# Attention block on one core: the weights of a Strassen group in one tile of seven blocks, in place of two tiles of four and three

## The chip, the cores and the metric

The kernel runs on 1 core of one Trainium2 chip. The metric is the device time in microseconds; the time of a kernel is the median of its runs.

## The reference

`x` has 16 images of 512 channels and 32 x 32 = 1024 positions, float32 throughout. One layer of self-attention with a group norm and a residual is computed:

```python
xn = group_norm(x, 8 groups, eps=1e-5) * norm_gamma + norm_beta
q, k, v = split(einsum('oc,bchw->bohw', qkv_w, xn) + qkv_b)      # each 512 x 1024 an image
# 4 heads of 128 channels
attn = softmax(q k^T / sqrt(128))                                 # 1024 x 1024 a head
out = attn v                                                      # back to 512 x 1024
out = einsum('oc,bchw->bohw', proj_w, out) + proj_b
return x + out
```

## The kernel before

**Attention.** The loop runs over steps: image `b`, head `h` of 4, key block `j` of 8 (128 keys). In a step TensorE makes a score tile of 128 keys by 1024 queries in two halves (`s`, L741), ScalarE takes its exponential (`p`, L746), VectorE adds it to a running sum (`tot`, L752 and L754), and TensorE adds V times `p` to the output's PSUM tile (`po`, L836), one step behind. At the end of a head VectorE makes the softmax's denominators (`denominators`, L763 to L777), whose inverses go to DRAM (`row`) and come back on all partitions (`rinv`); a head later VectorE multiplies the output by them (`divide`).

**Projections.** The q and k weights of two heads (a "pair"), the v weights and the output projection are each multiplied by Strassen's method in the Winograd form, on two levels: seven outer products, and in each of them seven inner ones. `two_levels` makes the units. The outer products come in four groups, `OUTER = ((1, 5), (2, 6), (7, 4), (3,))`; a group makes its one or two outer products side by side. In a group the inner products run in this order, the first operand of each being one block of weights (128 x 128 for each product of the group) and the second a block of x or of the heads' outputs (or a sum of such blocks, `in_t1` to `in_t4`, made by VectorE at L522):

```python
FACTORS = {
    1: ("a11", "b11"), 2: ("a12", "b21"), 3: ("s4", "b22"), 4: ("a22", "t4"),
    5: ("s1", "t1"), 6: ("s2", "t2"), 7: ("s3", "t3"),
}
ORDER = (1, 2, 6, 5, 7, 4, 3)
```

The products of one accumulator are copied by ScalarE (`kept_copy`, L448) and joined by VectorE (`out_`, L557), then combined over the groups (L593) and finished. The four sites are q and k of pair 0, of pair 1, v, and proj. Their groups are staggered: group 1 starts four units after group 0, and so on.

**Where the units stand.** `plan_head` lays them between the attention steps. In image b's head 0 stands pair 1 of the same image, in head 1 the output projection of the image before (and the load, the statistics and the normalisation of the next image's x), in head 2 pair 0 of the next image, in head 3 v of the next image, in seven of the eight key blocks. The Tile framework's scheduler orders the instructions of each engine from this; each engine then works in that order and waits on semaphores.

**Weights.** `group_weights` gives a group its blocks. In image 0 it makes them from the raw weights: blocks a11 to a22 by DMA or, for the outer sums, by VectorE, then s1 to s4 by VectorE. Then it writes them to DRAM (`kept`), and every later image reads them back with `nc.sync.dma_start`, whose queue (SP's) also carries the loads of v's kept sums `v_t` (L511, L588). The tile pool has two buffers of each tile, so a group's load waits until TensorE has read the last block of the same tile two groups before. A block's place is given by `SLOTS`; s3 takes the place of a21.

**Other DMA queues.** On POOL's stand the loads of x, of the residual (`y<-in_x`), the stores of the output (`out_y<-y`), the stores of the kept sums (`kept_t<-qk_t`) and the transposition of v by way of DRAM (`vd<-vu`, `v<-vd`); on ScalarE's `row` and `rinv`.

Of the kernel before, what the change touches and what calls it, by code (L numbers as in the profile page):

```python
# [10 lines left out]
F32 = mybir.dt.float32  # L11
# [5 lines left out]
P = 128  # L17
# [71 lines left out]
def attention_block(  # L89
# [52 lines left out]
FACTORS = {  # L142
    1: ("a11", "b11"), 2: ("a12", "b21"), 3: ("s4", "b22"), 4: ("a22", "t4"),
    5: ("s1", "t1"), 6: ("s2", "t2"), 7: ("s3", "t3"),
}


SLOTS = {
    "a11": (0, 0), "a12": (0, 1), "s1": (0, 2), "s2": (0, 3),
    "a21": (1, 0), "s3": (1, 0), "a22": (1, 1), "s4": (1, 2),  # L150
}
PARTS = (4, 3)
KC = 2
Q = 256

# [4 lines left out]
def fast_path(ctx, tc, x, sources, out, consts, flag, dims):  # L160
# [6 lines left out]
    nc = tc.nc  # L167
# [8 lines left out]
    wpool = ctx.enter_context(tc.tile_pool(name="w", bufs=2))  # L176
# [12 lines left out]
    kept = ctx.enter_context(tc.tile_pool(name="kept", bufs=1, space=DRAM))  # L189
# [120 lines left out]
    def load_block(dst, src):  # L310

        to = dst.rearrange("p (r k) d -> p r k d", k=KC)
        for k in range(KC):
            nc.sync.dma_start(
                to[:, :, k, :], src[ts(k, P), :].rearrange("p (r d) -> p r d", d=P)
            )

    stage, store = {}, {}
    for site in (*range(PAIRS), "proj", "v"):
        for g, group in enumerate(OUTER):  # L320
            for t, m in enumerate(PARTS):
                store[site, g, t] = kept.tile(
                    [P, len(group), m, P], F32, name=f"kept_{site}_{g}_{t}"
                )

    store["last"] = kept.tile([P, 8, HALF], F32, name="kept_last")

# [22 lines left out]

    def group_weights(site, g, first):


        group = OUTER[g]
        n = len(group)
        w = [
            wpool.tile([P, 2, m, P], F32, tag=f"w{t}", name=f"w{t}_{site}_{g}")
            for t, m in enumerate(PARTS)
        ]
        if not first:  # L360
            for t in range(2):
                nc.sync.dma_start(w[t][:, :n], store[site, g, t])
            return w
        st, raw = stage[site], raw_blocks(site)
        for i, p in enumerate(group):
            name = FACTORS[p][0]
            for t in range(2):
                rows = w[t][:, i, 0:2, :]
                flat = rows.rearrange("p s d -> p (s d)")
                if name in raw:  # L370
                    nc.sync.dma_start(
                        rows, raw[name][:, ts(t, P)].rearrange("(k p) d -> p k d", p=P)
                    )
                    continue

                def of(m):
                    return st[m][:, ts(t, 2 * P)]

                if name == "s1":
                    nc.vector.tensor_add(flat, of("a21"), of("a22"))  # L380
                elif name == "s2":
                    nc.vector.tensor_sub(flat, of("s1"), of("a11"))
                elif name == "s3":
                    nc.vector.tensor_sub(flat, of("a11"), of("a21"))
                else:
                    nc.vector.tensor_sub(flat, of("a12"), of("s2"))
            if site == "proj":
                for t in range(2):
                    nc.sync.dma_start(
                        store["last"][:, p, ts(t, 2 * P)],  # L390
                        w[t][:, i, 0:2, :].rearrange("p s d -> p (s d)"),
                    )

        def at(m):
            t, slot = SLOTS[m]
            return w[t][:, :n, slot, :]

        nc.vector.tensor_add(at("s1"), at("a21"), at("a22"))
        nc.vector.tensor_sub(at("s3"), at("a11"), at("a21"))
        nc.vector.tensor_sub(at("s2"), at("s1"), at("a11"))  # L400
        nc.vector.tensor_sub(at("s4"), at("a12"), at("s2"))
        for t in range(2):
            nc.sync.dma_start(store[site, g, t], w[t][:, :n])
        return w

    wv = {}
# [25 lines left out]
    def run(units):  # L432
        for u in units:
            u()
# [49 lines left out]
    def two_levels(name, site, b, blocks, finish, sums="make"):  # L484
# [10 lines left out]
        def group_units(g):  # L495
            group = OUTER[g]
            n = len(group)
            have = haves[g]

            def weights():  # L500
                have["w"] = group_weights(site, g, b == 0 and site in range(PAIRS))

            def sum_tile(h, m):
                haves[h][m] = tpool.tile(
                    [P, 2, Q], F32, tag=f"in_{m}", name=f"{name}_{h}_{m}"
                )
                return haves[h][m][:, : len(OUTER[h])]

            def load(h, m):
                if sums == "load" and h < len(OUTER):  # L510
                    nc.sync.dma_start(sum_tile(h, m), inner_kept[b, h, m])  # L511

            def inner_sum(m):
                if sums == "load":
                    return
                sum_tile(g, m)
                a, c = {
                    "t1": ("b12", "b11"), "t2": ("b22", "t1"), "t3": ("t2", "b11"),
                    "t4": ("b21", "t2"),
                }[m]  # L520
                for i in range(n):
                    nc.vector.tensor_sub(have[m][:, i, :], inner(i, a), inner(i, c))  # L522
                if sums == "keep":
                    t = dpool.tile([P, n, Q], F32, tag=f"{m}_{g}", bufs=1, name=f"kept_{m}_{g}")
                    inner_kept[b, g, m] = t
                    nc.gpsimd.dma_start(t, have[m][:, :n])  # L526

            def inner(i, m):
                if m[0] == "t":
                    return have[m][:, i, :]  # L530
                outer = blocks()[FACTORS[group[i]][1]]
                return outer[int(m[1]) - 1][:, ts(int(m[2]) - 1, Q)]

            def mm(acc, j, first):
                an, bn = FACTORS[j]
                t, slot = SLOTS[an]
                for i in range(n):
                    nc.tensor.matmul(  # L538
                        acc[:, ts(i, Q)], have["w"][t][:, i, slot, :], inner(i, bn),
                        start=(first and i == 0), stop=True, skip_group_check=True,  # L540
                    )

            def out_(which, a, c=None):
                row, half = int(which[1]) - 1, int(which[2]) - 1
                if g not in R:
                    R[g] = rpool.tile(
                        [P, 2, 2, HALF], F32, tag=f"r{g % 3}", name=f"{name}_r{g}"
                    )
                dst = R[g][:, :n, row, ts(half, Q)]

                def view(t):
                    return t[:, : n * Q].rearrange("p (i q) -> p i q", q=Q)

                if c is None:
                    nc.scalar.copy(dst, view(a))
                else:
                    nc.vector.tensor_add(dst, view(a), view(c))  # L557

            p1, p2, p6, p5, p7, p4, p3 = strassen(f"{name}_{g}", mm, out_, n * Q)

            def unit(*steps):
                def one():
                    for f in steps:
                        f()
                    for _ in range(min(len(pending), 2 if g == len(OUTER) - 1 else 1)):
                        pending.pop(0)()
                return one

            def end():
                combine(g)  # L570
                if g == len(OUTER) - 1:
                    run(pending)
                    pending.clear()


            return [
                unit(weights, lambda: inner_sum("t1"), lambda: inner_sum("t2"), p1),
                unit(lambda: inner_sum("t3"), p2), unit(lambda: inner_sum("t4"), p6),
                unit(lambda: load(g + 1, "t2"), p5), unit(lambda: load(g + 1, "t1"), p7),
                unit(lambda: load(g + 1, "t3"), p4),  # L580
                unit(lambda: load(g + 1, "t4"), p3, end),
            ]
# [17 lines left out]
        def combine(g):  # L600

            if g == 1:
                done("c11", (0, 0), (1, 0))
                add((1, 1), (0, 0), (1, 1))
                add((1, 0), (1, 1), (0, 1))
            elif g == 2:
                add((2, 0), (1, 1), (2, 0))
                done("c22", (2, 0), (0, 1))
                done("c21", (2, 0), (2, 1))
            elif g == 3:  # L610
                done("c12", (1, 0), (3, 0))
# [444 lines left out]
    for s in range(steps + 1):  # L1056
# [14 lines left out]
        for half in range(NH2):  # L1071
# [10 lines left out]
            n = (len(units) + 1) // 2  # L1082
# [137 lines left out]
```

## Time and profile before

| | |
|---|---|
| median of 3 runs | 3298.59 us (3294.85 to 3303.18) |
| the profiled execution's own time | 3294.85 us |
| its span, first to last instruction | 3293.0 us |
| TensorE matmuls busy | 3198.6 us, 97% |
| VectorE busy | 2639.3 us, 80% |
| ScalarE busy | 1443.6 us, 44% |
| GpSimd busy | 525.1 us, 16% |
| mean granted TensorE clock | 0.996 |
| DMA | 530.59 MB, mean 161 GB/s |

One execution was profiled. [...] A float32 matmul appears as two records. In the timeline a row gives the start, the time from the first start to the last end of the records that it merges, the engine, the line, the operation, the operands, and in brackets the idle time before it with what ended it. In the DMA issues a row ends in the size of one and the median time from issue to landing. In the waits a row gives the total, the number and the longest.

### The profile page before, as it was taken

The numbers are of one execution on the slowest core, as the hardware profiler recorded it, in microseconds if no ns is written. First come the engines' busy times: TensorE is split into PE (matmuls) and PEld (weight loads), VectorE is DVE, ScalarE is ACT, GpSimd is POOL, SyncE is SP. The second block draws the span as 40 slices with busy tenths as digits, with TensorE's granted clock in tenths as the row PEclk, the third lists the DMA queues.
The fourth block names the chain that finished last, engine by engine and source line by source line (L and its number), as shares of the span: only waits on it lengthen the run. The fifth ranks groups of instructions, "written<-read, shape, count | busy, mean of one in ns | idle before, by whom it ended". The sixth has DMA issues, their size and how long they took to land.

```text
span 3293.0 us, 34096 instructions
## 1 busy us (share of the span) xinstructions
PE 3198.6 (97%) x10474; PEld 2177.7 (66%) x10474; DVE 2639.3 (80%) x4625; ACT 1443.6 (44%) x2709; POOL 525.1 (16%) x938
## 2 busy tenths in 40 slices
PE   8999999999999999999999999999999999999999
PEld 6566666666666666666666666666666666666664
DVE  8878878778787787878888787887878878788684
ACT  2535435344353443534435354353533535344342
POOL 1011121111211112111121201212012120121100
PEclk9999999999999999999999999999999999999999
DMA  6554554545545455454554545546455463554631
GB/s 206 196 189 152 168 182 139 181 137 178 169 150 174 140 170 166 155 169 142 179 168 156 172 130 183 169 148 182 132 174 172 147 200 124 176 160 154 195 122 40
DMA packets 210539, 530.59 MB, mean 161 GB/s; under 512 B 33072, under 2 KB 66096, under 8 KB 210352
## 3 DMA queue, kind: packets, MB, share of 16 engines
q1 hardware_dynamic: 128992, 276.88, 27.2%
q0 software_dynamic: 67392, 216.07, 20.0%
q10 hardware_dynamic: 13968, 35.41, 3.1%
q8 instruction: 87, 1.43, 0.2%
q14 instruction: 100, 0.82, 0.1%
HBM read 389.56 MB, written 138.67 MB: 160 GB/s over the span
## 4 chain that ended last, share of the span: by engine, by line
issue 38%; PE 37%; DVE 11%; DMA 7%; POOL 5%; ACT 0%; POOLq 0%; SPq 0%; DVEq 0%
PE po L836 10%; PE s L741 10%; PE qk_x L538 5%; DMA vd<-vu 4%; POOL kept_t L526 4%; PE qk_y L538 4%; PE pp_x L538 4%; PE pp_y L538 3%; DMA out_y<-y 2%; DVE xt L277 2%; DMA y<-in_x 1%; DVE tot L754 1%; DVE vu L680 1%; DVE part L765 1%; DVE tt L763 1%
## 5 line engine op out<-in xcount | busy, mean ns | idle before, releaser
L836 PE MATMUL po<-p,v 128*128 128x512 f32 x2048 | 1056.6, 598 | 0.0
L741 PE MATMUL s<-qk,qk 128*128 128x512 f32 x2048 | 1052.8, 596 | 3.3 <-ACT p L746 3.2
L746 ACT ACTIVATE p<-s 128x512 f32<-128x512 f32 x1024 | 609.7, 596 | 851.6 <-PE s L741 810.0
L836 PEld LDWEIGHTS po<-p,v 128*128 128x128 f32 x2048 | 603.2, 303 | 328.2 <-issue 209.0
L754 DVE TENSOR_TENSOR tot<-tot,p 128x1024 f32<-128x1024 f32 x385 | 468.5, 1217 | 164.6 <-ACT p L746 162.6
L741 PEld LDWEIGHTS s<-qk,qk 128*128 128x128 f32 x2048 | 388.6, 191 | 106.4 <-issue 40.0
L538 PE MATMUL qk_x<-qk_t,w 128*128 128x256 f32 x1344 | 363.2, 387 | 43.0 <-DVE qk_t L522 38.6
L538 PEld LDWEIGHTS qk_x<-qk_t,w 128*128 128x128 f32 x1344 | 248.5, 191 | 211.9 <-issue 106.5
L448 ACT COPY qk_u<-qk_x 128x512 f32<-128x512 f32 (+1 forms) x256 | 136.1, 532 | 333.7 <-PE qk_x L538 286.7
L526 POOL DMA_DIRECT2D kept_t<-qk_t x256 | 138.3, 540 | 505.6 <-DVE qk_t L522 455.9
L688 POOL DMA_DIRECT2D vd<-vu x120 | 66.2, 552 | 747.5 <-DVE vu L680 745.8
L557 DVE TENSOR_TENSOR qk_r<-qk_y,qk_u 128x512 f32<-128x512 f32 (+1 forms) x256 | 158.3, 618 | 25.8 <-ACT qk_u L448 19.7
L538 PE MATMUL pp_x<-pp_t,w_proj 128*128 128x256 f32 x630 | 170.7, 387 | 6.4 <-ACT pp_p L448 6.4
L538 PE MATMUL v_x<-v_t,w_v 128*128 128x256 f32 x630 | 166.6, 381 | 0.0
L725 POOL DMA_DIRECT2D out_y<-y x120 | 66.2, 552 | 624.2 <-DVE y L724 591.6
L557 DVE TENSOR_TENSOR v_r<-v_y,v_u 128x512 f32<-128x512 f32 (+1 forms) x120 | 74.5, 621 | 112.5 <-ACT v_u L448 82.3
L538 PEld LDWEIGHTS pp_x<-pp_t,w_proj 128*128 128x128 f32 x630 | 113.9, 190 | 76.3 <-issue 22.5
L538 PEld LDWEIGHTS v_x<-v_t,w_v 128*128 128x128 f32 x630 | 118.5, 190 | 53.6 <-issue 23.0
L538 PE MATMUL qk_y<-x,w 128*128 128x256 f32 x512 | 144.4, 384 | 9.4 <-DVE qk_r L557 9.3
L693 POOL DMA_DIRECT2D v<-vd x240 | 139.9, 590 | 79.3 <-issue 67.1
L752 DVE TENSOR_TENSOR tot<-p,p 128x1024 f32<-128x1024 f32 x64 | 78.3, 1223 | 78.4 <-ACT p L746 78.4
L448 ACT COPY v_u<-v_x 128x512 f32<-128x512 f32 (+1 forms) x124 | 66.2, 534 | 165.1 <-PE v_x L538 126.2
(204 smaller groups left out, 4524.8 us busy)
## 6 DMA issues: line engine op xcount, KB each, us to landing
kept_t<-qk_t POOLq DMA_DIRECT2D x192, 256.0 KB, 3.5
w<-kept SPq DMA_DIRECT2D x90, 512.0 KB, 4.0
v_t<-kept_t SPq DMA_DIRECT2D x180, 256.0 KB, 3.0
w<-kept SPq DMA_DIRECT2D x90, 384.0 KB, 3.8
rinv<-row ACTq DMA_DIRECT2D x63, 512.0 KB, 5.5
x<-in_x POOLq DMA_DIRECT2D x60, 512.0 KB, 4.9
vd<-vu POOLq DMA_DIRECT2D x120, 256.0 KB, 3.4
v<-vd POOLq DMA_DIRECT2D x240, 128.0 KB, 4.5
```

Of the source, the lines that this page charges most:

```text
L448: nc.scalar.copy(t[n][:, :width], t["x"][:, :width])
L526: nc.gpsimd.dma_start(t, have[m][:, :n])
L538: nc.tensor.matmul(acc[:, ts(i, Q)], have["w"][t][:, i, slot, :], inner(i, bn), start=(first and i == 0), stop=True, skip_group_check=True,)
L557: nc.vector.tensor_add(dst, view(a), view(c))
L688: nc.gpsimd.dma_start(rows[which][ts(h, P), :], u)
L693: nc.gpsimd.dma_start(vs[b, pair][ts(q, BLK), half].rearrange("m h (k i) j -> m (h k) (i j)", k=n), rows[which].rearrange("(k m) (q e) -> ...
L725: nc.gpsimd.dma_start(out[b, ts(o, P), ts(half, HALF)], t)
L741: nc.tensor.matmul(sc, ks[b, h][:, ts(j, P)], qs[b, h][:, ts(half, HALF)], start=True, stop=True)
L746: nc.scalar.activation(ps[s][:, ts(half, HALF)], sc, AF.Exp, scale=SCALE)
L752: nc.vector.tensor_add(tot[b, h], ps[s - 1], ps[s])
L754: added[b, h, j] = nc.vector.tensor_add(tot[b, h][:, i], tot[b, h][:, i], ps[s][:, i])
L836: nc.tensor.matmul(po[b, h][:, i], v_block(b, h, j), ps[s][:, i], start=(j == 0), stop=(j == NB - 1),)
```

## The change

The two tiles `w0` and `w1` of a group become one tile `w` of seven blocks. In place of a load of 512 KB and one of 384 KB for a group of two products (half of that for the group of one) there is one load of 896 KB (448 KB) from one DRAM tile; so too for the stores in image 0. The outer sums of image 0 are made in one VectorE instruction of 512 columns in place of two of 256, and the raw blocks are loaded by `load_block`, in two DMAs as before, but cut by rows and not by columns. TensorE's, ScalarE's and GpSimd's instructions are the same in number. The stores of `store["last"]`, two for each block, become one.

```diff
-SLOTS = {
-    "a11": (0, 0), "a12": (0, 1), "s1": (0, 2), "s2": (0, 3),
-    "a21": (1, 0), "s3": (1, 0), "a22": (1, 1), "s4": (1, 2),
-}
-PARTS = (4, 3)
+SLOTS = {"a11": 0, "a12": 1, "a21": 2, "s3": 2, "a22": 3, "s1": 4, "s2": 5, "s4": 6}
...
         for g, group in enumerate(OUTER):
-            for t, m in enumerate(PARTS):
-                store[site, g, t] = kept.tile(
-                    [P, len(group), m, P], F32, name=f"kept_{site}_{g}_{t}"
-                )
+            store[site, g] = kept.tile(
+                [P, len(group), 7, P], F32, name=f"kept_{site}_{g}"
+            )
...
         group = OUTER[g]
-        n = len(group)
-        w = [
-            wpool.tile([P, 2, m, P], F32, tag=f"w{t}", name=f"w{t}_{site}_{g}")
-            for t, m in enumerate(PARTS)
-        ]
+        w = wpool.tile([P, 2, 7, P], F32, tag="w", name=f"w_{site}_{g}")
         if not first:
-            for t in range(2):
-                nc.sync.dma_start(w[t][:, :n], store[site, g, t])
+            nc.sync.dma_start(w[:, : len(group)], store[site, g])
             return w
...
-        for t in range(2):
-            nc.sync.dma_start(store[site, g, t], w[t][:, :n])
+        nc.sync.dma_start(store[site, g], w[:, : len(group)])
         return w
...
             def mm(acc, j, first):
                 an, bn = FACTORS[j]
-                t, slot = SLOTS[an]
                 for i in range(n):
                     nc.tensor.matmul(
-                        acc[:, ts(i, Q)], have["w"][t][:, i, slot, :], inner(i, bn),
+                        acc[:, ts(i, Q)], have["w"][:, i, SLOTS[an], :], inner(i, bn),
                         start=(first and i == 0), stop=True, skip_group_check=True,
                     )
```

In the built program the order of TensorE's instructions in the images from the second on differs in one place an image: in head 2, a score and a weighted sum (half a key block each) stand ahead of the first product of pair 0's group 2, not behind it. ScalarE's order follows by one place; VectorE's and GpSimd's there are the same.

More of the change, by code (lines that the diff above doesn't have):

```diff
@@ L365, in group_weights, with at @@
         for i, p in enumerate(group):
-            name = FACTORS[p][0]
-            for t in range(2):
[L368 to L386, printed above, removed]
-            if site == "proj":
[L388 to L396, printed above, removed]
+            n = FACTORS[p][0]
+            flat = w[:, i, 0:4, :].rearrange("p s d -> p (s d)")
+            if n in raw:
+                load_block(w[:, i, 0:4, :], raw[n])
+            elif n == "s1":
+                nc.vector.tensor_add(flat, st["a21"], st["a22"])
+            elif n == "s2":
+                nc.vector.tensor_sub(flat, st["s1"], st["a11"])
+            elif n == "s3":
+                nc.vector.tensor_sub(flat, st["a11"], st["a21"])
+            else:
+                nc.vector.tensor_sub(flat, st["a12"], st["s2"])
+            if site == "proj":
+                nc.sync.dma_start(store["last"][:, p], flat)
+        def at(n):
+            return w[:, : len(group), SLOTS[n], :]
         nc.vector.tensor_add(at("s1"), at("a21"), at("a22"))
@@ L401, in group_weights @@
         nc.vector.tensor_sub(at("s4"), at("a12"), at("s2"))
-        for t in range(2):
-            nc.sync.dma_start(store[site, g, t], w[t][:, :n])
+        nc.sync.dma_start(store[site, g], w[:, : len(group)])
         return w
```

## The prediction

> **What bounds the kernel now.** I read the page's first part, then its chain, then SP's waits, then the engines' timelines around the weight loads.
>
> ```profile
> PE 3198.6 (97%) x10474; PEld 2177.7 (66%) x10474; DVE 2639.3 (80%) x4625; ACT 1443.6 (44%) x2709; POOL 525.1 (16%) x938
> ...
> issue 38%; PE 37%; DVE 11%; DMA 7%; POOL 5%; ACT 0%; POOLq 0%; SPq 0%; DVEq 0%
> ```
>
> TensorE is busy 97% of the span, and three quarters of the chain is its own work and issue. So a microsecond by which TensorE waits longer is a microsecond of time, and nothing else counts unless it ends up as such a wait. Taking from each matmul's start the usual pitch (0.43 us for 512 columns, 0.215 for 256), I find about 142 us lost in the whole span, 7 to 9 us in nearly every full batch. None of the large pieces waits for weights. Three recur, all behind VectorE: 2.3 to 2.9 us at the start of head 0 (outer group 0 of pair 1 waits for `qk_t`), 0.8 us in head 3 at `v_r`, and in head 2, in outer group 0 of the next batch's pair 0, about 0.4 + 0.3 + 0.7 us.
>
> The weights are read from DRAM once a group. SP issues each load as soon as the tile's last reader, two groups earlier, is done:
>
> ```profile
> SPq L362 <- PE qk_y L538: 980.8, 195, 10.8
> SPq L362 <- PE pp_y L538: 600.7, 88, 9.2
> ```
>
> So a load's start is set by TensorE's release and its end must come before the group's first product. Both tiles start to move early: the 512 KB tile goes after product 5 of the older group, the 384 KB tile after product 3, and the smallest lead I find from a 512 KB landing to its first use is 6.1 us (2.2 us at the first such loads, in batch 0). This is the slack that the change spends.
>
> **One tile: the release moves to the older group's last product, the need stays at the new group's first.** Products run in the order 1, 2, 6, 5, 7, 4, 3. With one tile of seven slots the load starts where today the 384 KB load starts, and must land before product 1, where today only the 512 KB load must. What lies between is a window of other TensorE work that I can read, since TensorE's order after the change is the same but for one place a batch. For 11 of the 16 places (four sites by four groups) the windows are 9.3 us and more: nothing waits. Tight are pair 0's group 1 (5.20 us), and group 2 of v, of pair 1 and of proj (5.86 us each), and above all group 2 of pair 0. In one batch:
>
> ```profile
> 1394.72 0.32 SPq L362 DMA_DIRECT2D w<-kept  x1
> ```
>
> ```profile
> 1397.18 1.03 PE L538 MATMUL qk_x<-qk_t,w 128*128 128x256 f32 x4
> 1398.05 1.03 PE L538 MATMUL qk_x<-xt,w 128*128 128x256 f32 x4
> 1398.91 1.02 PE L741 MATMUL s<-qk,qk 128*128 128x512 f32 x2
> 1399.77 1.02 PE L836 MATMUL po<-p,v 128*128 128x512 f32 x2
> ```
>
> The release is at 1394.72, the group's first product at 1398.05: 3.3 us (3.35 in the median batch). In the built order of the changed kernel the score and the weighted sum of 1398.91 and 1399.77 stand ahead of that product, which adds 2 x 0.86: 5.07 us. From every window goes 0.19 us, because the weight load on the array precedes the matmul.
>
> **How long 896 KB take.** No transfer of that size is in the trace, so its price has bounds. The nearest rows:
>
> ```profile
> w_proj<-kept_proj SPq DMA_DIRECT2D x45, 512.0 KB, 3.5
> ...
> w_proj<-kept_proj SPq DMA_DIRECT2D x45, 384.0 KB, 3.0
> ```
>
> In the quiet proj site 128 KB more cost 0.5 us, which for the missing 512 KB would be 2.0. The page's queue q1 moved 276.88 MB in 27.2% of 16 engines' span, 309 GB/s, which makes 1.7 us. The bare packets of 4 KB last 0.159 us and each engine gets 8 of them: 1.3 us. Where other queues take half of the engines it is twice that, 2.5 us. The low end is 0.85 us, if the load that today runs beside the 384 KB one (the next group's 512 or 256 KB tile, which will start later) gives back a third of 1.3. How busy the engines are at the places is in the windows:
>
> ```profile
> 1493.00:1499.00 6.00, 6.00 (x22) 4.25 (x21) 4.92 (x10) 1.99 (x4) 2.14 (x4) 1.00 0.98 370
> 1394.70:1398.50 3.80, 3.80 (x15) 2.82 (x15) 3.48 (x8) 0.85 (x2) 1.10 (x3) 1.00 0.90 306
> 1375.80:1380.80 5.00, 5.00 (x16) 3.25 (x15) 4.12 (x8) 2.51 (x5) 1.08 (x2) 1.00 0.65 211
> ```
>
> The column before the last is the DMA share. At pair 1's group 2 (first row, beside the next batch's x, the residual's y and the broadcast `rinv`) it is 0.98; at pair 0's group 2 0.90; at its group 1 0.65. So I take 2.0, 1.5 and 1.3 us, and add each to what the 384 KB load took there.
> - Pair 0, group 2: 384 KB took 4.18 us in the median batch (2.9 to 4.9). 4.18 + 1.5 + 0.03 for the issue less 4.88 is 0.83; over the 15 batches, each with its own row, 15 us.
> - Pair 0, group 1: 3.77 + 1.3 + 0.03 less 5.01: 0.1 in the median, 3 us in all.
> - Pair 1, group 2: 3.1 to 5.4 us, median 3.94; plus 2.0 less 5.67: 0.3 in the median, but 1 to 2 in some batches and more in the last, 10 us in all.
> - Group 2 of v and proj: 3.1 + 1.3 against 5.67: nothing (spare 1.2 us).
>
> New waits: 28 us. With 0.85 us everywhere the same sum makes 9, with 1.3 20, with 2.0 46, with 2.5 68.
>
> [...]
>
> **What the early loads cost today, and what comes back.** They fall on other transfers. In head 2 the 512 KB load of group 1 is issued at 1368.25, 0.15 us ahead of the output's stores:
>
> ```profile
> 1368.40 1.16 POOL L725 DMA_DIRECT2D out_y<-y  x2 [6.44 <-DVE y L724]
> ...
> 1373.27 1.18 POOL L712 DMA_DIRECT2D y<-in_x  x2 [2.14 <-DMA out_y<-y]
> ```
>
> ```profile
> 1376.68 0.75 DVE L721 SCALAR_TENSOR_TENSOR y<-pp_r,projb_sb,y 128x512 f32<-128x512 f32 x1 [1.31 <-DMA y<-in_x]
> ```
>
> The store took 4.6 us where undisturbed ones take 2.3; POOL's next load waits for its buffer, and VectorE for that load: 18.6 us in all (`DVE y L721 <- DMA y<-in_x`, 20 times). That idle time does reach TensorE: in the batch where VectorE waited twice (1.20 + 1.05 us, at 964 to 967) TensorE's wait a few microseconds later was 1.45 us, not the usual 0.4. Without the early load the first wait of 0.4 us should vanish in about 12 batches (5 us), and a third of the 0.7 us at `qk_r`, which follows VectorE's waits for `kept_t` stores beside the 512 KB load of group 2 (5 us): 10 us together. Bounds: nothing, if the stores are slow for another reason; 20 us, if all three waits there go. At the start of head 0 the 512 KB load at 1057.30 stands beside `vd<-vu`, for which VectorE waits 5.9 us in 15 batches (`DVE vt L677`); TensorE's long wait follows in the chain, so 6 us come back. Bounds: 4 us of loss, if the bigger load 4 us later delays the next stores, and 12 of gain, if the shorter wait also spares some of the half-clock stretches. The matmuls after it show one: 2.04 us for four where 1.03 is usual, at 1072.10; the clock is halved in eight stretches of 3.4 us among the full batches, some 1.7 us each.
>
> **The rest.** SP's queue: the single load stands in the built order where the 384 KB load stood, ahead of the same `v_t` loads, so nothing new queues behind its wait; if it did, v's sums would pay up to a window's shortfall, under 1 us. On VectorE 32 half-width sums of batch 0 (0.42 us each) become 16 whole ones (0.68), 2.6 us less, beside other work. Raw loads of the first groups now wait for product 3: about 0.5 us at group 2 in the prologue, where no attention work fills in. I take 1 us for the first batch, between -1 and 3. Of SP's issues 0.32 us each go, off the path.
>
> **Sum.** 28 + 1 - 10 - 6 = 13 us on the profiled execution's 3294.85 (span 3293.0, 1.85 around it): 3307.9. The median of before, 3298.59, is 3.7 above that execution, so the forecast is 3311, 0.4% slower. About 0.3%, 10 us, is what a measurement of this kernel can tell from no change.
>
> **Rivals.** *The halves cancel.* The extra bytes cost 1.3 us everywhere, as bare packets (20 us), and 16 come back: +5, 3303. For it: TensorE's order grew by 1.72 us just where it is tightest. Against: DMA shares of 0.90 and 0.98. *Faster.* One mechanism: VectorE, freed of the early 512 KB loads, no longer trails TensorE in head 2 and at head 0's start, 20 + 6 + 5 for spared half clocks, against 9 of new waits and 1: -21, 3278. It decides once the extra is under about 1.2 us and all three waits in head 2 go; for it speaks the doubled wait of one batch, against it that VectorE has enough other work there. *Much slower.* The extra is 2.5 us: 68 + 1 - 16 = +53, 3352; or at 2.0, +31, 3330.
>
> **How the numbers follow.** Slower, with the forecast at 3311 and the extreme at 3352: 0.45. Within 10 us: 0.31. Faster: 0.24. The range leaves about a tenth on each side: from 3284, in the faster case, to 3338, between the extras of 2.0 and 2.5.
>
> **What would show it.** Right: new rows in TensorE's waits at the first product of group 2 in pair 0 and pair 1, released by DMA w<-kept, some 0.8 and 0.7 us a batch; one load of 896 KB at 5 to 6 us; VectorE's wait for y<-in_x near zero. Wrong: no TensorE wait on w<-kept at all, a load under 4.5 us in head 2, or y's wait unchanged; and waits for weights at v or proj would mean that the load is far slower than any bound here.

## The result, and the profile after

| | before | after |
|---|---|---|
| median (lowest to highest), us | 3300.89 (3294.85 to 3303.83) | 3283.01 (3279.09 to 3288.52) |
| profiled execution (its span), us | 3294.85 (3293.0) | 3283.12 (3281.3) |

The ratio of the times is 0.9949, with a 95% interval of 0.9928 to 0.9971: the change made the kernel 0.5% faster. The forecast was 3311 us, 0.4% slower; 3283 us lies just under its range, which began at 3284, and next to the time of the rival called *Faster*, 3278.

The page of the changed kernel, its lines on busy time, packets, the queue of the weight loads, the chain and the loads themselves (KB of one, median us from issue to landing):

```profile
PE 3188.9 (97%) x10474; PEld 2177.4 (66%) x10474; DVE 2636.7 (80%) x4609; ACT 1447.4 (44%) x2709; POOL 526.9 (16%) x938
...
DMA packets 172663, 530.54 MB, mean 162 GB/s; under 512 B 28864, under 2 KB 51904, under 8 KB 172480
...
q1 hardware_dynamic: 91120, 276.86, 25.8%
...
PE 74%; DVE 15%; DMA 6%; issue 2%; ACT 2%; POOL 0%; SPq 0%; DVEq 0%; POOLq 0%; ACTq 0%
...
w<-kept SPq DMA_DIRECT2D x90, 896.0 KB, 5.2
...
w_proj<-kept_proj SPq DMA_DIRECT2D x45, 896.0 KB, 4.5
```

TensorE is still the bound (97%), with the same count of matmuls. The chain's 74% for PE and 2% of issue stand where before had 37% and 38%; both sum to three quarters, so this is the same work under other names. Of the chain's 6% for DMA, 5 are `w<-kept` by its line. One load of 896 KB takes 4.5 to 5.2 us in the median, against 3.5 and 3.0 for the two of before in proj.

The waits, by total us, number and longest; first SP's own, which time the loads, then the engines', and last three rows of before that they are compared with:

```profile
SPq L350 <- PE qk_y L510: 1340.5, 119, 22.8
```

```profile
PE qk_x L510 <- DVE qk_t L495: 29.2, 16, 2.0
PE qk_x L510 <- DMA w<-kept: 22.4, 16, 2.4
...
DVE qk_t L495 <- DMA kept_t<-qk_t: 12.0, 8, 2.3
...
DVE y L693 <- DMA y<-in_x: 4.0, 9, 0.9
```

```profile
PE qk_x L538 <- DVE qk_t L522: 38.6, 30, 2.8
...
PE qk_y L538 <- DVE qk_r L557: 9.6, 14, 2.4
...
DVE qk_t L522 <- DMA kept_t<-qk_t: 10.8, 17, 2.3
```

SP now has little more than half as many waits for its weight tiles, one a group, for product 3 of the older group. Two things stand beside each other. TensorE has a row that it did not have, waits for `w<-kept`, 22.4 us. And the rows that it paid for before are smaller: its wait for `qk_t` fell from 38.6 to 29.2 us, its wait for `qk_r` from 9.6 to 0.5, and VectorE's wait for `y<-in_x` fell from 18.6 to 4.0. VectorE's wait for `kept_t` kept its sum, 10.8 us before and 12.0 after, but not its place. Before, 11 of 17 waits stand 17 to 19 us after the first projection product of head 2, where TensorE waits behind them for `qk_r`; after, all eight stand 21 to 24 us after it, just ahead of TensorE's new wait.

The new wait is where the prediction put it, in head 2 at the first product of pair 0's group 2. The timeline of TensorE and SP there:

```profile
1384.35 0.32 SPq L350 DMA_DIRECT2D w<-kept  x1
...
1386.80 1.03 PE L510 MATMUL qk_x<-qk_t,w 128*128 128x256 f32 x4
1387.66 1.02 PE L713 MATMUL s<-qk,qk 128*128 128x512 f32 x2
1388.52 1.02 PE L808 MATMUL po<-p,v 128*128 128x512 f32 x2
1391.88 1.10 PE L510 MATMUL qk_x<-xt,w 128*128 128x256 f32 x4 [2.33 <-DMA w<-kept]
```

The score and the weighted sum stand ahead of the product, as built, and still TensorE stops for 2.33 us: the load is issued at 1384.35 and the product starts at 1391.88.

Now the other side, POOL and VectorE earlier in head 2, where before had stores from 1368.40 on that took 4.6 us:

```profile
1359.32 1.16 POOL L697 DMA_DIRECT2D out_y<-y  x2 [6.45 <-DVE y L696]
...
1362.05 0.54 POOL L684 DMA_DIRECT2D y<-in_x  x1
...
1362.82 0.54 POOL L684 DMA_DIRECT2D y<-in_x  x1 [0.23 <-DMA out_y<-y]
...
1366.60 0.75 DVE L693 SCALAR_TENSOR_TENSOR y<-pp_r,projb_sb,y 128x512 f32<-128x512 f32 x1 [0.30 <-DMA y<-in_x]
```

From the first stores to the first load that reuses a buffer are 2.7 us (1359.32 to 1362.05), where before needed 4.87 (1368.40 to 1373.27). VectorE waits 0.30 us and not 1.31. At the start of head 0, TensorE's long wait is shorter:

```profile
1271.59 1.47 PE L510 MATMUL qk_x<-qk_t,w 128*128 128x256 f32 x4 [1.81 <-DVE qk_t L495]
```

And at pair 1's group 2, where the prediction feared a full DMA, and at pair 0's group 2, the windows, placed against the load's issue as the prediction's were (the column before the last is the DMA share):

```profile
1486.47:1492.47 6.00, 6.00 (x22) 4.25 (x21) 3.76 (x7) 1.78 (x3) 2.15 (x4) 1.00 0.75 262
...
1384.40:1388.00 3.60, 3.60 (x13) 2.53 (x13) 3.54 (x9) 0.73 (x2) 1.08 (x2) 1.00 1.01 356
```

The first was 0.98 before and is 0.75; the second was 0.90 and is 1.01.

**An account by place.** As for the 142 us of the prediction, I took from each matmul's start the usual pitch and summed what is left, by place, over the 14 full batches between the first and the last (us; worked out from the starts in the traces, slow clock included):

| place | before | after |
|---|---|---|
| head 2, pair 0 group 0 | 28.1 | 1.5 |
| pair 0 group 1, first products | 0.0 | 1.3 |
| pair 0 group 2, first product | 0.0 | 23.9 |
| start of head 0 (pair 1 group 0) | 51.0 | 41.4 |
| pair 1 group 2 and the rest of head 0 | 1.2 | 1.2 |
| v | 14.9 | 14.7 |
| proj group 3 | 13.4 | 11.9 |
| prologue and first batch | 17.0 | 18.1 |
| whole span (with small pieces and the last batch) | 141.9 | 129.2 |

12.7 us less, beside 11.7 us less span. The medians are 17.9 us apart: the profiled execution of before was its fastest, so the account covers some 12 of them. The change is a trade in head 2, 26.6 us given back at group 0 for 25.2 of new waits at groups 1 and 2, and the profit lies at head 0's start, 9.6 us, and in proj, 1.6. The difference in proj comes from one batch, where TensorE's wait for `pp_p` was 1.5 us and not 0.4.

### The profile page after: what moved, and what is told of

It is laid out like the page before. It is cut to its first block, busy times and chain, and to the rows that moved or that the text cites. A ratio compares the mean times of both kernels' runs of the same rounds, so it can differ in the third digit from the quotient of the medians.

```text
span 3281.3 us, 33566 instructions
## 1 busy us (share of the span) xinstructions
PE 3188.9 (97%) x10474; PEld 2177.4 (66%) x10474; DVE 2636.7 (80%) x4609; ACT 1447.4 (44%) x2709; POOL 526.9 (16%) x938
## 2 busy tenths in 40 slices
DMA packets 172663, 530.54 MB, mean 162 GB/s; under 512 B 28864, under 2 KB 51904, under 8 KB 172480
## 3 DMA queue, kind: packets, MB, share of 16 engines
q1 hardware_dynamic: 91120, 276.86, 25.8%
## 4 chain that ended last, share of the span: by engine, by line
PE 74%; DVE 15%; DMA 6%; issue 2%; ACT 2%; POOL 0%; SPq 0%; DVEq 0%; POOLq 0%; ACTq 0%
PE po L808 20%; PE s L713 20%; PE qk_x L510 11%; PE qk_y L510 7%; DMA w<-kept 5%; PE pp_x L510 4%; PE v_x L510 4%; PE v_y L510 3%; PE pp_y L510 3%; DVE vu L652 3%; DVE tot L726 2%; DVE vt L649 2%; ACT x L82 1%; DVE v_r L565 1%; DVE v_r L529 1%
## 5 line engine op out<-in xcount | busy, mean ns | idle before, releaser
L510 PE MATMUL qk_x<-qk_t,w 128*128 128x256 f32 x1344 | 361.0, 385 | 31.6 <-DVE qk_t L495 29.2
L597 DVE SCALAR_TENSOR_TENSOR qk<-qk_r,qkb_sb,qk_r 128x512 f32<-128x512 f32 x192 | 137.0, 740 | 1.1
```

The source lines that it names most:

```text
L510: nc.tensor.matmul(acc[:, ts(i, Q)], have["w"][:, i, SLOTS[an], :], inner(i, bn), start=(first and i == 0), stop=True, skip_group_check=True,)
L597: nc.vector.scalar_tensor_tensor(st[b, h][:, ts(half, HALF)], a, qkb_sb[:, i : i + 1], c, ALU.add, ALU.add)
```

## The experiments

*Theory 1*: the early 512 KB loads of before slow transfers that VectorE waits for, and VectorE then holds TensorE: group 1 of pair 0 slows the `out_y` stores, group 2 of pair 0 the `kept_t` stores, group 1 of pair 1 the `vd` loads. The lateness helps; the tile's being one does not matter for it. *Theory 2*: it is the merge itself, one request with rows of 7168 bytes in place of two with 4096 and 3072. The first six experiments leave the two tiles of before and only make early loads late. Times come with the ratio to before on the same chip and its 95% interval.

### All early loads late, two tiles kept (e1_late_all)

```diff
         if not first:
+            if True:
+                second = nc.sync.dma_start(w[1][:, :n], store[site, g, 1])
+                with tc.issue_after(second.ins):
+                    nc.sync.dma_start(w[0][:, :n], store[site, g, 0])
+                return w
             for t in range(2):
```

> Two tiles as before, but the 512 KB load stands behind the 384 KB load in SP's queue for every group, so both start only after product 3 of the older group, as the single load does. Theory 1, the moment: what came back came from taking the early 512 KB load away from beside the stores and loads that VectorE waits for. Then this runs as the one-tile kernel: 3283 +- 6 us, waits of pair 0's group 0 in head 2 under 3 us over the 14 middle batches (28 before, 1.5 after), and 20 to 30 us of waits for weights at pair 0's group 2. Theory 2, the merge: it came from one transfer with longer packets (172663 packets in place of 210539). Then the early load's cost stays: group 0's waits 20 us and more, no less than 3298 us.

Measured: 3296.06 us, 0.9986 (0.9972 to 0.9999).

```profile
PE qk_x L543 <- DMA w<-kept: 20.0, 21, 2.6
...
DVE y L726 <- DMA y<-in_x: 5.2, 11, 1.7
...
DVE qk_t L527 <- DMA kept_t<-qk_t: 2.2, 6, 0.6
```

The relief came without the merge: `y<-in_x` and `kept_t` hardly hold VectorE, and group 0 of pair 0 loses 1.1 us where before lost 28.1. That is theory 1. But the time missed what was expected. The two late loads land later than the one in other places: 5.51 us after the release at pair 1's group 2 (4.71 with one tile), which brought 7 us of waits there, and 6.09 at v's group 2 (4.61), 5 us, where a `v_t` load is issued between the two; head 0's start lost 7.6 us more than with one tile; at pair 0's group 2 they landed sooner, 5.71 (6.53), for waits of 15 us. So lateness is not all: with it alone 0.14% is gained, with the merge 0.51%. Whether the difference is the single request's or the order's, as at v's group 2, this run does not tell.

### Group 1 of pair 0 alone late (e2_late_g1)

```diff
-            if True:
+            if (site, g) == (0, 1):
```

> Two tiles as before, but for pair 0's group 1 alone the 512 KB load stands behind the 384 KB load. Theory 1: VectorE's wait for the residual's load (18.6 us before) falls under 5, of TensorE's 28 us in pair 0's group 0 the two first pieces go and the last, behind the kept_t stores, stays: about 12 us left, no wait for weights at group 2, the start of head 0 as before; 3284 to 3291 us. Theory 2: no change, 3297 to 3303.

Measured: 3284.57 us, 0.9956 (0.9943 to 0.9968).

```profile
DVE qk_t L527 <- DMA kept_t<-qk_t: 12.3, 17, 1.8
PE qk_y L543 <- DVE qk_r L562: 11.5, 12, 1.8
...
DVE y L726 <- DMA y<-in_x: 3.5, 8, 0.9
```

One 512 KB load an image, issued a few microseconds later, gives as much as the whole change (0.9949, with the two intervals overlapping). VectorE's wait for `y` goes from 18.6 to 3.5 us and TensorE's loss at group 0 from 28.1 to 14.9; against it stand 3.7 us of new waits at group 1's own first product. The waits for `kept_t` and `qk_r` stay, so they belong to another load.

### All late but group 2 of pair 0 (e3_late_not_g2)

```diff
-            if True:
+            if (site, g) != (0, 2):
```

> Two tiles, the 512 KB load behind the 384 KB load for every group but pair 0's group 2, which keeps its early 512 KB load. Theory 1: the gains of the one-tile kernel at head 0's start and at group 0 stay, less some 9 us for VectorE's waits on the kept_t stores beside the early load of group 2, and the 24 us of waits at group 2 go: 3263 to 3273 us, faster than both. Theory 2: 3297 to 3303.

Measured: 3290.27 us, 0.9976 (0.9966 to 0.9987). A miss. I had expected the best of both, no wait for weights at group 2 and little loss at group 0. The first came true (0.0 us), but group 0 lost 16.3 us, for the early load of group 2 that was left in by itself makes more than half of that loss: e1, with that load late too, lost 1.1. And v paid 4.5 us of waits, as in e1.

### Group 2 of pair 0 alone late (e5_late_g2)

```diff
-            if True:
+            if (site, g) == (0, 2):
```

> Two tiles; for pair 0's group 2 alone the 512 KB load stands behind the 384 KB load. Theory 1 (the early loads slow what VectorE waits for, each its own part): the early load of group 1 keeps its 11 to 13 us of waits at group 0, the part behind the kept_t stores (about 15 us) goes, and 15 us of waits for weights come at group 2, as with all loads late: 3296 to 3303 us, no change. Rival: group 1's and group 2's early loads act together and either alone gives all of it back: then group 0's waits fall under 5 us.

Measured: 3326.3 us, 1.0080 (1.0067 to 1.0094).

```profile
PE qk_x L543 <- DMA w<-kept: 24.3, 14, 2.4
DVE y L726 <- DMA y<-in_x: 17.9, 25, 1.2
...
DVE qk_t L527 <- DMA kept_t<-qk_t: 1.3, 4, 0.6
```

The mirror of e2: the wait for `kept_t` goes from 10.8 to 1.3 us, the one for `y` stays, and group 0 loses 16.7 us, 11.4 less than before. Together with e2's 13.2 that makes 24.6 of the 26.6 us that the change gave back there, and each load has its own wait. The time was missed, by 23 us above the range: the two loads landed 7.10 us after the release (I had taken the 5.71 of e1), and the waits at group 2's first product made 26.5 us. There were also sixteen stretches of 3.4 us with half the clock, against eight in before. Why these loads were slower here than in e1 was not tried. The trace shows one difference: a third load, the 256 KB of group 3, is still early here and is issued 0.9 us after the release (at 1400.64, for a release at 1399.71), while in e1 it is issued more than 11 us after it. That this is the cause is likely, and not shown.

### Group 1 of pair 1 alone late (e6_late_pair1_g1)

```diff
-            if True:
+            if (site, g) == (1, 1):
```

> Two tiles; for pair 1's group 1 alone the 512 KB load stands behind the 384 KB load, which takes it away from beside the vd stores at the start of head 0. Theory 1: TensorE's wait there falls from 2.45 to about 2.05 us a batch, VectorE's wait for vd from 5.9 to under 2 us; 51 us of losses at head 0's start become 40 to 45, all else stays: 3290 to 3296. Rival: that gain comes with all loads being late or with the merge: 2.4 us and 3297 to 3303.

Measured: 3294.8 us, 0.9973 (0.9961 to 0.9986).

```profile
PE qk_x L543 <- DVE qk_t L527: 34.5, 30, 3.0
...
DVE vt L682 <- DMA vd<-vu: 2.5, 4, 1.0
```

VectorE's wait for `vd` falls from 5.9 to 2.5 us, and TensorE's stall at head 0's start from 2.45 to 2.02 us a batch in the median, exactly the 2.02 of the changed kernel. (It stays at 2.38 to 2.43 in e2, e5 and e8, where this load is early.) So the shorter stall does not need the merge. By sum it is 4 us of the 7 that the change gave back in the stall, since in four batches it was still 2.3 to 3.1 us. By the account this execution lost 49.5 us at head 0's start, only 1.5 less than before and short of the 40 to 45 expected; seven stretches of half clock fell there, where before had six, so the clock's share of the gain is not shown by this run.

### Group 2 of pair 1 alone late (e8_late_pair1_g2)

The prediction put 10 us of new waits at this place and they did not come; this run asks what had made the DMA full there.

```diff
-            if True:
+            if (site, g) == (1, 2):
```

> Two tiles; for pair 1's group 2 alone the 512 KB load stands behind the 384 KB load. It asks why the one-tile kernel has no waits for weights at pair 1's group 2, where 10 us were predicted from the crowded transfers of before. Theory 1: the crowd was made by the group's own early 512 KB load; without it the 384 KB load there takes 3.1 to 3.3 us (median 3.9 before), and both have landed 5.4 to 5.6 us after the release, as with all loads late; waits there at most 8 us, 3298 to 3308 us in all. Rival: the crowd comes from the next image's x and from rinv, and eased in the one-tile kernel only because other groups' loads moved: then the 384 KB load still takes 3.8 us and more and the waits exceed 10 us.

Measured: 3305.68 us, 1.0004 (0.9994 to 1.0015).

TensorE waited once for weights at this place, 1.6 us. The 384 KB load took 3.17 us in the median, where it took 3.94 in before, and both tiles had landed 5.38 us after the release, inside the 5.83 us to the first product. The early load is not itself in the crowd: in all 15 batches of before it had landed 0.2 to 3.9 us ahead of the 384 KB load's issue. It is issued some 10 us ahead of it, and `rinv` after it, in one batch of before:

```profile
1484.11 0.32 SPq L362 DMA_DIRECT2D w<-kept  x1
```

```profile
1490.77 0.33 ACTq L790 DMA_DIRECT2D rinv<-row  x1
```

```profile
1493.58 0.32 SPq L362 DMA_DIRECT2D w<-kept  x1
```

By the packets in the traces, in the first 3.4 us after the 384 KB load's issue the weights had 0.36 of the DMA engines in before, POOL's queue 0.26 and `rinv`'s 0.25. In e8 the weights had 0.64, POOL's queue 0.06 and `rinv`'s nothing. `rinv` landed 2.7 us after that issue in the median of before, and 0.1 us after it in e8. So the crowd at this place was `rinv` and POOL's transfers, and the group's own 512 KB load had held them back into it; the change takes that load away (`rinv` then lands 0.3 us after the issue). The median alone would be weak: in e5, e6 and e2, which leave this load early, it is 3.33, 3.46 and 4.01 us. But one 384 KB load of 15 took more than 3.6 us in e8, and five to eleven in before and these three.

### One tile, its third group planned later (e7_one_tile_later1, e4_one_tile_later)

The changed kernel with more of TensorE's other work between the release and the first product of pair 0's group 2: the plan's start for the third group goes from 8 to 9 (e7) or 10 (e4).

```diff
-    def staggered(lists):
+    def staggered(lists, third=8):
...
-        starts = (0, 4, 8, 16)[: len(lists)] if len(lists) != 3 else (0, 4, 10)
+        starts = (0, 4, third, 16)[: len(lists)] if len(lists) != 3 else (0, 4, 10)
...
-            spread(plan, staggered(qk_groups(b + 1, 0)), 0, NB)
+            spread(plan, staggered(qk_groups(b + 1, 0), 10), 0, NB)
```

> The one-tile kernel, with group 2 of pair 0 starting one unit later (9 in place of 8), which puts 0.86 us more of TensorE's work between release and first product. If the window sets the wait, the 24 us of waits there fall by 0.86 a batch, to 10 to 13 us: 3269 to 3275 us, between the one-tile kernel and two units later.

> The one-tile kernel, with group 2 of pair 0 starting two units later (10 in place of 8), which puts 2 to 3 us more of TensorE's work between the release of its tile and its first product. Theory 1 with the window as the cause of the 24 us: those waits fall under 6 us and nothing takes their place, 3262 to 3270 us. Rival: the wait for weights only stands where VectorE would make TensorE wait anyway; then waits on VectorE take its place and the time stays within 5 us of 3283.

Measured: e7 3266.43 us, 0.9894 (0.9879 to 0.9909), below the range expected; e4 3266.64 us, 0.9902 (0.9888 to 0.9916). Both beat before and after. The waits for weights, in e7:

```profile
PE qk_x L510 <- DMA w<-kept: 8.0, 10, 1.5
```

and in e4, where VectorE's wait for `y<-in_x` stays about as small as in the changed kernel (5.1 and 4.0 us):

```profile
PE qk_x L510 <- DMA w<-kept: 0.6, 1, 0.6
```

The work between release and first product is 5.16 us in the changed kernel, 6.02 in e7 and 8.60 in e4; the loss at that product 23.9, 10.7 and 0.0 us. Growing the window by 0.86 us in 14 batches should take 12 us, and 13.2 went: the new wait is the load's landing less the window, as the prediction had it. Taking away the last 10.7 us brought little: the medians of e7 and e4 are level, and over the whole span the account of e4 is only 3.4 us lower (111.2 against 114.6), for other waits took their place in part, among them 3.1 us for `qk_r` where e7 has 0.5.

### The change again (e9_one_tile_again)

No edit; the changed kernel beside a later group of runs.

> The changed kernel again, to measure it beside the kernel before on one chip: theory 1 and its rivals all expect 3283 +- 4 us and a ratio of 0.993 to 0.997, with waits for weights at pair 0's group 2 of 20 us or more in the profile.

Measured: 3286.08 us, 0.9949 (0.9934 to 0.9964), with 23.3 us lost at pair 0's group 2 and 43.0 at head 0's start. The ratio is the first one again.

### One tile, loaded in two requests (e10_one_tile_two_dmas)

```diff
-            nc.sync.dma_start(w[:, : len(group)], store[site, g])
+            for i in range(len(group)):
+                nc.sync.dma_start(w[:, i : i + 1], store[site, g][:, i : i + 1])
```

> One tile as in the change, but each full group's load is issued as two DMAs of 448 KB one behind the other (rows of 3584 bytes in place of 7168), both at the release of the whole tile. It tells apart what made the one load land sooner after the release than the two late loads of the run in which all early loads were made late (4.71 us against 5.51 at pair 1's group 2, 4.61 against 6.09 at v's group 2). If it is the single DMA with its long rows, the second half lands at 5.2 us or later at pair 1's group 2 and at 5.3 or later at v's group 2, head 0's first group gets longer loads too, and the time lies at 3288 to 3296. If it is the place in SP's queue, since the loads late in that run stood with others between them, the landings stay within 0.35 us (0.32 of it the second issue) of the one load's, the waits for weights at pair 0's group 2 are 20 to 32 us, and the time is 3281 to 3288.

Measured: 3296.66 us, 0.9984 (0.9972 to 0.9996).

```profile
PE qk_x L511 <- DMA w<-kept: 25.6, 20, 2.9
```

The time is 0.7 us above the range expected if the single request matters, and it is that of e1. Where the comparison is clean the landings agree with that: at pair 1's group 2 the second half landed 5.58 us after the release (the two tiles of e1 5.51, the one request 4.71), at proj's group 1 5.60 against 4.46; at the quiet group 2 of proj there is no difference, 4.45 and 4.52. But not all of the expectation came true: at pair 0's groups 1 and 2 and pair 1's group 0 the two halves landed a little sooner (4.42, 5.98, 5.76 against 4.92, 6.53, 5.99). And the run is not clean everywhere. A product's first matmul now waits for its half alone, so the built order moved in the first batch (7.5 us more lost there, and 2.2 in the prologue) and at pair 0's group 2, and a `v_t` load fell between the halves at v's group 2. So of the 12 us between this run and the change some 10 may be order, by the account of an execution that was itself 6 us above its median. The time is therefore no evidence for the single request; what is shown is the landing at pair 1's group 2 and at proj's group 1, not the price.

## Why the prediction was wrong, step by step

- **What bounds the kernel, and what would move**: right. The loads start at the release of product 3, the waits for weights appear at group 2 of pair 0, `y<-in_x` falls near zero, SP's queue brings no wait. The windows were right: 5.07 us predicted at group 2 of pair 0, 5.16 measured.
- **Head 2's gain, "10 us together"**: the term that failed. It was 26.6 us. The mechanism was the one named; the size was not. I let two thirds of VectorE's late waits go unpaid, "a third of the 0.7 us at `qk_r`", because VectorE "has enough other work there". e2 gives 13.2 us for the load beside the `out_y` stores alone, and e5 11.4 for the load beside the `kept_t` stores. The sum holds a slip as well: a third of 0.7 us in 14 batches is 3.3 us, not 5. Even the upper bound of 20 was too low, as it counted the three waits at their usual length (they sum to 22.2 us) and not the slower matmuls right behind them (at 1387.09 of before four took 1.13 us where 1.03 is usual), with which 28.1 us are lost there.
- **Pair 1's group 2, 10 us of new waits**: failed. There was no such wait in the 14 batches, only 1.1 us in the last. I added 2.0 us to the 384 KB load's time because the DMA share was 0.98, and took that crowd as given. But the change moves the group's own 512 KB load, which had held `rinv` and POOL's transfers back into the window (e8: 3.94 us became 3.17); over the same stretch the share is now 0.75. The load took 4.71 us, 0.77 more than the 384 KB load. That the load running beside it "gives back a third" is not borne out here: two late loads landed 5.38 us after the release with it (e8) and 5.51 without (e1).
- **Pair 0's group 2, 15 us of new waits**: 23.9 us. The load took 6.53 us there and not 4.18 + 1.5: the extra was 2.35. The DMA share is 1.01 at that place, and here the crowd stayed: by the packets, POOL's queue had 0.46 of the engines in the first 3.5 us after the load's issue, 0.41 in before. e7 and e4 show that the wait follows the window.
- **Pair 0's group 1, 3 us**: 1.3 us, and the extra 1.15 us beside the 1.3 taken. v and proj: nothing, as said (4.61 and 4.52 us).
- **Head 0's start, 6 us back**: 9.6 us. 7.0 of it is the shorter stall (37.4 to 30.4 us), of which e6 ties 4 to the 512 KB load beside `vd<-vu`; the other 2.6 goes with fewer half-clock stretches, four at this place where six were. (Of the eight stretches that the prediction put into the full batches one stood in the first batch and one in head 2.) Clock was counted only in the rival.
- **First batch, 1 us**: 1.1 with the prologue. Proj's 1.6 us were not foreseen. They came back in e1 and e3 too, and not in e2, e5, e6 and e8, so they need no merge; no run isolates the load.

Summed: 16.6 more came back in head 2, 7.2 more was paid at pair 0's groups 1 and 2, 8.9 less at pair 1's group 2, 3.6 more came back at head 0 and 1.6 in proj: 23.5 us, which turns the predicted +13 into -10, beside the 11.7 us less of the two spans (the rest is in small pieces). The rival *Faster* named this mechanism and its sign, 20 + 6 + 5 against 10. Its condition was half wrong: nearly all the waits at group 0 in head 2 did go (1.5 us are left), but the extra was not under 1.2 us where it counted, and the relief was large enough to pay for it. That its 3278 lies close is partly luck: it had 9 us of new waits where 25 came, and less relief than came.

The load took 4.5 us in the median in the quiet proj site, and 6.53 at pair 0's group 2, where the DMA share was 1.01 in the batch shown. Starting a load early did not pay here: in e2 the later issue of one load a batch made the kernel 0.44% faster, since its data were not needed early and what it slowed was (VectorE's wait for `y` went from 18.6 to 3.5 us).

**What stays open.** Late loads alone leave some 12 us of the gain out (e1 against the change), and e10 shows that the single request lands sooner at pair 1's group 2. How much of the 12 us is the merge's and how much the order's is not shown; whether the single request lands sooner by its longer packets or by having no second request behind it was not told apart, nor why the two late loads of e5 took 7.10 us.

## What to carry to other kernels

Before moving a load later, list which stores and loads stand beside it today and who waits for those: a transfer that is early "for free" may be paid by another engine, and the bill comes where that engine next holds the bound one (here 28.1 us of TensorE's time at group 0 in head 2, and 1.5 after the change). When pricing a bigger load in a crowded window, do not take the crowd as given: a load that moves away lets what it held up finish earlier, here `rinv`, which landed 2.7 us after the 384 KB load's issue in before and 0.1 in e8, and POOL's transfers, whose share after that issue went from 0.26 to 0.06. And price both sides by all the time lost at a place, not by the one wait that is easiest to name; then look whether the new wait can be covered by planning its reader a little later, which here was worth as much again (0.990 against 0.995).

## What was not expected of the hardware

- The load with rows of 7168 bytes moved in packets of 7168 bytes, 272 ns each in the median, where the two loads of before moved in packets of 4096 bytes, 159 ns, and of 3072, 121 ns: packets fell from 210539 to 172663, and q1's share from 27.2% to 25.8% for the same bytes.
- Half the clock came after some waits of under 3 us, and not after others as long. The execution of before has eight stretches of 3.4 us at half the clock: one in the first batch, one in head 2 and six at head 0's start, where the 15 stalls are 2.3 to 2.9 us long. The one of after has five, one in the first batch and four at head 0's start, with stalls of 2.0 to 2.1 us. e5, with long waits at two places a batch, had sixteen: eleven at head 0's start, four at pair 0's group 2, one in the first batch. Of before's 15 stalls the six with such a stretch lasted 2.4 to 2.8 us, and the longest, 2.9 us, had none; what decides it is not shown.
